# Axial attention on one core: the maximum ahead of the reciprocal, GpSimd copying the turned weights by position, ScalarE scaling three of four strips

## The chip, the core and the metric

The kernel runs on one core of one Trainium2 chip. Its time is the device time of one execution in microseconds (us); of several executions the median is given. The engines are called as in the profile: PE (TensorE), DVE (VectorE), ACT (ScalarE), POOL (GpSimd) and SP (SyncE, which here only issues DMAs). [...]

## The reference

Four layers are computed one after another on an input of 2 x 128 x 128 x 128 (image, channel, row, column) in float32. The change touches the first one alone, an attention along the rows of each column, in eight groups of channels. Cut to what matters:

```python
qkv = _bn(jnp.einsum('bgch,gdc->bgdh', xg, wg), ...)        # per column: q, k (8 each), v (16)
qr = jnp.einsum('bgci,cij->bgij', q, q_emb)                  # q against position embeddings
kr = jnp.einsum('bgci,cij->bgij', k, k_emb).swapaxes(2, 3)
qk = jnp.einsum('bgci,bgcj->bgij', q, k)
sim = _bn(jnp.concatenate([qk, qr, kr], 1), ...).reshape(NW, 3, GROUPS, H, H).sum(1)
sim = jax.nn.softmax(sim, axis=3)
sv = jnp.einsum('bgij,bgcj->bgci', sim, v)                   # weights times values
sve = jnp.einsum('bgij,cij->bgci', sim, v_emb)               # weights times embeddings
so = _bn(jnp.concatenate([sv, sve], -1).reshape(NW, OUT * 2, H), ...)
out = so.reshape(N, W, OUT, 2, H).sum(3)
```

Here `bgij` has one 128 x 128 matrix for each column and group. There are 2 x 128 columns and 8 groups, so 2048 such matrices. A recurrent layer of convolutions, a deformable convolution and a convolution by transforms follow; nothing in them is changed.

## The kernel before, in words

`layer0_prepare` projects q, k and v and stores them in device memory. `layer0_attention` then makes the 2048 matrices. A **unit** is one image, one group and 32 neighbouring columns (64 units). A unit is done in four **pairs** of eight columns each, two rows of `RT` = 4, so there are 256 pairs. One pass of the loop `for m in range(pairs + 14)` handles several pairs at once, each in another phase, and issues the work of all of them in an order written out by hand: the wrapper `InOrder` (line 81 of the kernel, to which the profile books nearly every instruction) keeps each engine's queue in program order. In pass m:

- `logits_pe(u, p)`: PE turns the term `r[0]` into the PSUM tile `lg` (eight transposes) and adds the products of q and k (`lg<-qk`). `add_term`: DVE adds the other term `r[1]` and writes `e` (128 x 1024).
- `maxima`: DVE reduces `e` to the negated maximum `mx` of each row. `exponentials`: ACT applies the exponential in eight pieces, each with its sum into `total`.
- `divide`, one pass later: DVE takes the reciprocal of `total`, POOL multiplies `e` by it.
- `turn`, two passes later: PE transposes the weights `e` in two halves (r = 0, 1) into the PSUM tile `te`, of which there is one buffer. `turned`: ACT copies each half into `u.et`, by position (row, then column). `turned_v`: DVE copies each half into `et`, in the order in which it stands in PSUM.
- `values`, three passes later: PE multiplies `et` by the values `vt` (`po<-et,vt`), and ACT copies the result to `svt`.
- `embedded_pe`, six passes later: PE multiplies `u.et`, by position, by the value embeddings `ve` (`po<-et,ve`, 32 small products a pass), and ACT copies the result to `ste` in `embedded_copy`.
- `terms_pe`: PE makes a quarter of the embedding products of the next unit in the PSUM tile `gen`, which has four strips of 512 elements. `terms_copy` scales them into `r[0]` or `r[1]`: ACT takes strips 2 and 3, DVE then strips 0 and 1.
- `stats`: DVE takes batch statistics (`bn_stats`) of a half of `svt` or `ste`, one each pass. SP loads `zz`, `vt` and `qk` for later units and stores `svt` and `ste`.

The PSUM tiles `gen`, `lg`, `te` and `po` have one buffer each: PE can fill one again only when its readers are done. `po` serves the values and the embeddings in turn. The tile `et` has two buffers and `e` four.

Of the kernel before, what the change touches and what calls it, by code (L numbers as in the profile page):

```python
# [7 lines left out]
F32 = mybir.dt.float32  # L8
# [7 lines left out]
P = 128  # L16
N = 2
S = 128
RT = 4
# [527 lines left out]
def layer0_attention(env, prm, mem, alphas, mv):  # L547
# [12 lines left out]
    pe, dve, act, pool, sync = (  # L560
        InOrder(tc, e) for e in (nc.tensor, nc.vector, nc.scalar, nc.gpsimd, nc.sync)
    )
    ident = env.ident
    HW = WC // 2
    with ExitStack() as ctx:
# [3 lines left out]
        ep = ctx.enter_context(tc.tile_pool(name="at_e", bufs=3))  # L569
# [3 lines left out]
        st_v, st_e = (  # L573
            cp.tile([P, NG, N * NC, 2, 6], F32, name=f"st_so{k}", tag=f"st_so{k}")
            for k in range(2)
        )
# [20 lines left out]
        units = [(n, g, wc) for n in range(N) for g in range(NG) for wc in range(NC)]  # L597
# [28 lines left out]
        def terms_pe(u, t, k):  # L626

            if k == 0:
                u.r[t] = rp.tile([P, WC, S], F32, name=f"r{t}", tag=f"r{t}")
            ps = pp.tile([P, 4, 4, 4, WC], F32, name="gen", tag="gen")  # L630
            for b in range(4):
                for s in range(4):
                    pe.matmul(
                        ps[:, s, b],
                        lhsT=toep[32 * s : 32 * s + 32, t, 4 * k + b, :],
                        rhs=u.z[32 * s : 32 * s + 32, t, :, 4 * k + b, :],
                        start=True,
                        stop=True,
                    )
            return ps  # L640

        def terms_copy(u, t, k, ps, s):

            to = u.r[t].rearrange("p w (s i) -> p s w i", s=4)
            to = to[:, s : s + 2, :, 16 * k : 16 * k + 16]
            here = ps[:, s : s + 2].rearrange("p s b i w -> p s w (b i)")
            scale = alphas[:, u.g, 1 + t : 2 + t]
            if s == 0:
                dve.tensor_scalar(to, here, scale, None, ALU.mult)
            else:  # L650
                act.activation(to, here, AF.Copy, scale=scale)

        def logits_pe(u, p):

            lg = pp.tile([P, 2, RT, S], F32, name="lg", tag="lg")
            for r in range(2):
                for x in range(RT):
                    pe.matmul(
                        lg[:, r, x, :],
                        lhsT=u.r[0][:, (2 * p + r) * RT + x, :],  # L660
                        rhs=ident,
                        is_transpose=True,
                        start=(x == 0),
                        stop=False,
                        skip_group_check=True,
                    )
            for x in range(RT):
                for r in range(2):
                    lo = u.base + 32 * r
                    w = p * RT + x  # L670
                    pe.matmul(
                        lg[:, r, x, :],
                        lhsT=qk[lo : lo + 8, 0, w, :],
                        rhs=qk[lo : lo + 8, 1, w, :],
                        start=False,
                        stop=(x == RT - 1),
                        skip_group_check=True,
                    )
            return lg

        def add_term(u, p, lg):
            e = ep.tile([P, 2 * RT, S], F32, name="e", tag="e", bufs=4)
            dve.tensor_tensor(
                e,
                lg.rearrange("p r x j -> p (r x) j"),
                u.r[1][:, 2 * p * RT : 2 * (p + 1) * RT, :],
                ALU.add,
            )
            return e

        def maxima(e):
            mx = ep.tile([P, 2 * RT], F32, name="mx", tag="mx")
            dve.tensor_reduce(mx, e, AX.X, ALU.max, negate=True)
            return mx
# [13 lines left out]
        def divide(e, total):  # L708
            dve.reciprocal(total, total)
            pool.tensor_tensor(  # L710
                e, e, total.unsqueeze(2).to_broadcast([P, 2 * RT, S]), ALU.mult
            )

        def turn(e, r):

            te = pp.tile([P, RT, S], F32, name="te", tag="te")
            for x in range(RT):
                pe.transpose(te[:, x, :], e[:, r * RT + x, :], ident)
            return te

        def turned(u, p, r, te):
            w0 = (2 * p + r) * RT
            if w0 == 0:
                u.et = rp.tile([P, S, WC], F32, name="et2", tag="et2")
            act.copy(u.et[:, :, w0 : w0 + RT], te.rearrange("p w i -> p i w"))

        def turned_v(et, r, te):
            dve.tensor_copy(et[:, r * RT : (r + 1) * RT, :], te)

        def values(u, p, et):  # L730

# [26 lines left out]
        def embedded_copy(u, k):  # L758
            if k == 0:
                u.sve = sp.tile([P, WC, WC], F32, name="ste", tag="ste")  # L760
            act.copy(u.sve[:, 8 * k : 8 * k + 8, :], po_e)
# [5 lines left out]
        def store_sve(u):  # L767
            for s in range(4):
                sync.dma_start(
                    out=sve[u.g, s, :, u.n, u.wc],  # L770
                    in_=u.sve[32 * s : 32 * s + 16].rearrange("p i w -> p (i w)"),
                )

        def stats(u, st, t, half):
            dve.bn_stats(
                st[:, u.g, u.n * NC + u.wc, half, :],
                t.rearrange("p a b -> p (a b)")[:, 512 * half : 512 * half + 512],
            )
# [4 lines left out]
        pairs = 4 * len(units)  # L783
        us, es, ets, totals = {}, {}, {}, {}
# [3 lines left out]
        for t in range(2):  # L788
            for k in range(2):
                ps = terms_pe(us[0], t, k)  # L790
                for s in (0, 2):
                    terms_copy(us[0], t, k, ps, s)
        for m in range(pairs + 14):
            here = m < pairs
            u, p = us.get(m // 4), m % 4
            nxt = us[m // 4 + 1] if m // 4 + 1 < len(units) else None
            turning = 0 <= m - 2 < pairs
            if here:
                lg = logits_pe(u, p)
                es[m] = add_term(u, p, lg)  # L800
            if m - 1 in totals:
                divide(es[m - 1], totals.pop(m - 1))
            if turning:
                ub, pb = us[(m - 2) // 4], (m - 2) % 4
                e = es.pop(m - 2)
                ets[m - 2] = ep.tile([P, 2 * RT, S], F32, name="et", tag="et", bufs=2)
                te = turn(e, 0)
                turned(ub, pb, 0, te)
                turned_v(ets[m - 2], 0, te)
            if 0 <= m - 3 < pairs:  # L810
                values(us[(m - 3) // 4], (m - 3) % 4, ets.pop(m - 3))
            if here:
                mx = maxima(es[m])
            if nxt and here:
                ps = terms_pe(nxt, p // 2, p % 2)
                for s in (2, 0):
                    terms_copy(nxt, p // 2, p % 2, ps, s)
            piece = m - 6
            if 0 <= piece < pairs:
                embedded_pe(us[piece // 4], piece % 4)  # L820
                embedded_copy(us[piece // 4], piece % 4)
            if turning:
                te = turn(e, 1)
                turned(ub, pb, 1, te)
                turned_v(ets[m - 2], 1, te)
            if here:
                totals[m] = exponentials(es[m], mx)

            for st, k, half in ((st_v, 7, 0), (st_v, 8, 1), (st_e, 10, 0), (st_e, 13, 1)):
                if m >= k and (m - k) % 4 == 0 and (m - k) // 4 < len(units):  # L830
                    done = us[(m - k) // 4]
                    stats(done, st, done.sv if st is st_v else done.sve, half)
            if m % 4 == 3 and m // 4 + 2 < len(units):
                us[m // 4 + 2] = load(m // 4 + 2)
            if m >= 4 and m % 4 == 0 and m // 4 + 1 < len(units):
                load_qk(us[m // 4 + 1])
            if m % 4 == 3 and m >= 7 and (m - 7) // 4 < len(units):
                store_sv(us[(m - 7) // 4])
            if m % 4 == 2 and m >= 10 and (m - 10) // 4 < len(units):
                store_sve(us[(m - 10) // 4])  # L840
            if m % 4 == 1 and m >= 13 and (m - 13) // 4 < len(units):
                us.pop((m - 13) // 4)
        for g in range(NG):
            for k, st in enumerate((st_v, st_e)):
                dve.bn_aggr(mv[:, g, k, :], st[:, g].rearrange("p e f k -> p (e f k)"))
# [1056 lines left out]
```

## Time and profile before

| | us |
|---|---|
| median of 3 executions | 5850.1 |
| lowest and highest | 5849.14, 5858.86 |
| the profiled execution, its time | 5858.64 |
| its span | 5856.4 |
| attention loop, from the first add to the last statistics | about 494 to 2051 |
| one pass of the loop, mean from 700 to 1900 us | 6.01 |

The profile shows one execution. "Busy" is the time in which an engine executes; a line of a timeline gives start, duration, engine, source line, operation, output and inputs, shapes and count, and in brackets the idle time before it with what ended it. A line of the waits gives who waited for whom, the total in us, how often, and the longest. Durations of neighbouring instructions on one engine overlap by about 0.1 us, so the start-to-start time is less than the duration.

### The profile page before, as it was taken

How to read it: one execution, taken by the hardware profiler on the slowest of the kernel's cores; microseconds unless marked ns; L12 is line 12 of the kernel's file. 1: busy time of each engine (PE TensorE's matmuls, PEld its weight loads, DVE VectorE, ACT ScalarE, POOL GpSimd, SP SyncE). 2: the span in 40 equal slices, each digit the busy share in tenths (PEclk: the TensorE clock that was granted, in tenths of full speed). 3: DMA queues.
4: the chain of work that ended last, by engine and by line, in shares of the span. 5: the costliest groups of instructions: out<-in, count | busy, mean ns of one | idle time of the engine just before them, and what ended most of it. 6: DMA issues, size and time to landing. Idle time of an engine off the chain costs nothing. (4 is left out here: it accounts for less than half of the span.)

```text
span 5856.4 us, 162646 instructions
## 1 busy us (share of the span) xinstructions
PE 5399.6 (92%) x67323; PEld 4843.0 (83%) x67323; DVE 3930.1 (67%) x7273; ACT 2784.2 (48%) x8408; POOL 778.5 (13%) x727
## 2 busy tenths in 40 slices
PE   8997999999999804999999999999899999998999
PEld 8866777777777704999999999973799999998888
DVE  3646999999999845555555556653566666666887
ACT  1156999999999845443223330012233333333221
POOL 2112333333333221000000003320000000000000
PEclk9998999999999956999999999999899999999999
DMA  3243222222222284000000001114766777663000
GB/s 143 96 192 98 58 61 58 58 57 57 57 59 59 47 344 155 1 2 1 1 1 1 1 1 44 38 45 124 93 88 88 87 87 89 88 88 55 38 39 40
DMA packets 411365, 401.02 MB, mean 68 GB/s; under 512 B 63232, under 2 KB 368256, under 8 KB 397952
## 3 DMA queue, kind: packets, MB, share of 16 engines
q1 hardware_dynamic: 406160, 380.65, 30.6%
q8 instruction: 541, 8.86, 0.7%
q10 hardware_dynamic: 4464, 9.86, 0.5%
q14 instruction: 200, 1.64, 0.1%
HBM read 251.00 MB, written 139.37 MB: 67 GB/s over the span
## 5 line engine op out<-in xcount | busy, mean ns | idle before, releaser
L81 PE MATMUL pl<-ln,wl 128*128 128x128 f32 (+1 forms) x10160 | 1239.0, 276 | 9.0 <-DVE ln L81 8.2
L81 PEld LDWEIGHTS pl<-ln,wl 128*128 128x128 f32 x10160 | 1175.7, 190 | 20.3 <-issue 7.3
L81 ACT ACTIVATE e<-e,mx 128x128 f32<-128x128 f32 x2048 | 793.6, 395 | 0.4 <-DVE mx L81 0.4
L81 ACT COPY sm<-ps_s 128x432 f32<-128x432 f32 (+1 forms) x768 | 318.4, 487 | 817.3 <-PE ps_s L81 817.3
L81 POOL TENSOR_TENSOR e<-e,total 128x1024 f32<-128x1024 f32 x256 | 485.9, 1898 | 1092.2 <-DVE total L81 1092.2
L81 ACT COPY res<-ln 128x128 f32<-128x128 f32 x762 | 262.7, 345 | 720.1 <-DVE ln L81 720.1
L81 DVE COPY s<-ps_w 100x1152 f32<-100x1152 f32 x256 | 346.5, 1354 | 317.7 <-PE ps_w L81 317.7
L81 PE MATMUL ps_s<-s,xw 100*128 100x144 f32 x4096 | 545.2, 286 | 0.4 <-ACT sm L81 0.3
L81 PE MATMUL po<-sm,wdef 128*128 128x256 f32 x2304 | 539.2, 379 | 0.0
L81 PE MATMUL pl<-ln,ws 128*128 128x128 f32 x4064 | 537.1, 273 | 0.0
L81 PEld LDWEIGHTS ps_s<-s,xw 100*128 100x128 f32 x4096 | 517.2, 190 | 0.9 <-ACT sm L81 0.9
L81 DVE TENSOR_TENSOR v<-pl,c 128x128 f32<-128x128 f32 x508 | 148.2, 292 | 542.7 <-PE pl L81 542.7
L81 PEld LDWEIGHTS pl<-ln,ws 128*128 128x128 f32 x4064 | 494.9, 191 | 0.0
L81 PEld LDWEIGHTS po<-sm,wdef 128*128 128x128 f32 x2304 | 419.8, 190 | 47.6
L81 PE MATMUL m<-x,weff 128*128 128x256 f32 x2048 | 444.2, 380 | 14.8 <-DVE x L81 14.8
L81 PEld LDWEIGHTS m<-x,weff 128*128 128x128 f32 x2048 | 390.4, 191 | 68.3 <-issue 14.8
L81 DVE COPY et<-te 128x512 f32<-128x512 f32 x512 | 351.9, 687 | 85.3 <-ACT et L81 84.7
L81 ACT ACTIVATION_READ_ACCUMULATOR e<-e,mx 128x1 f32 x2048 | 397.7, 194 | 0.0
L81 DVE SCALAR_TENSOR_TENSOR ln<-v,res 128x128 f32<-128x128 f32 x1016 | 343.9, 339 | 49.0 <-DVE v L81 1.3
L81 PE MATMUL te<-cst_main,e 128*128 128x128 f32 x2048 | 334.8, 286 | 41.2 <-DVE et L81 33.8
L81 PE MATMUL gen<-zz,toep 32*128 32x128 f32 x8192 | 333.6, 289 | 19.9 <-DMA zz<-qb_d 12.1
L81 DVE TENSOR_SCALAR r<-gen,alphas 128x1024 f32<-128x1024 f32 x256 | 327.1, 1278 | 28.5 <-DMA qk<-qa_d 14.7
(225 smaller groups left out, 8317.6 us busy)
## 6 DMA issues: line engine op xcount, KB each, us to landing
xw<-px_d SPq DMA_DIRECT2D x1280, 80.0 KB
xa<-in_x SPq DMA_DIRECT2D x16, 1024.0 KB
v_d<-vs SPq DMA_DIRECT2D x16, 1024.0 KB
qb_d<-sb SPq DMA_DIRECT2D x16, 1024.0 KB
qa_d<-sa SPq DMA_DIRECT2D x8, 2048.0 KB
zz<-qb_d SPq DMA_DIRECT2D x1024, 16.0 KB
vt<-v_d SPq DMA_DIRECT2D x64, 256.0 KB
qk<-qa_d SPq DMA_DIRECT2D x256, 64.0 KB
```

Source lines behind the costliest of these rows:

```text
L81: return lambda *a, **k: self.tc.keep_in_program_order(issue(*a, **k))
```

## The change

Three things are changed in the loop, and one follows from them.

- `maxima` stands ahead of `divide`, and both stand after the first `turn` with its copy. Before, the reciprocal came first and the maximum last.
- ACT no longer copies the halves of `te`. DVE's copy of them into `et` is the only reader, and POOL then copies `et` to `u.et`, by position, both halves at once (`by_position`). The embedding products and what comes after them are a pass later, so the loop is one pass longer.
- ACT scales strips 1 to 3 of `gen`, DVE strip 0.
- Of the statistics and stores, those of `ste` move by one pass.

```diff
@@ terms_copy
+            part = slice(0, 1) if s == 0 else slice(1, 4)
             to = u.r[t].rearrange("p w (s i) -> p s w i", s=4)
-            to = to[:, s : s + 2, :, 16 * k : 16 * k + 16]
-            here = ps[:, s : s + 2].rearrange("p s b i w -> p s w (b i)")
+            to = to[:, part, :, 16 * k : 16 * k + 16]
+            here = ps[:, part].rearrange("p s b i w -> p s w (b i)")
@@
-        def turned(u, p, r, te):
-            w0 = (2 * p + r) * RT
-            if w0 == 0:
+        def turned(et, r, te):
+            dve.tensor_copy(et[:, r * RT : (r + 1) * RT, :], te)
+
+        def by_position(u, p, et):
+
+            if p == 0:
                 u.et = rp.tile([P, S, WC], F32, name="et2", tag="et2")
-            act.copy(u.et[:, :, w0 : w0 + RT], te.rearrange("p w i -> p i w"))
-
-        def turned_v(et, r, te):
-            dve.tensor_copy(et[:, r * RT : (r + 1) * RT, :], te)
+            lo = 2 * p * RT
+            pool.tensor_copy(u.et[:, :, lo : lo + 2 * RT], et.rearrange("p w i -> p i w"))
@@ the loop
-        for m in range(pairs + 14):
+        for m in range(pairs + 15):
...
-            if m - 1 in totals:
-                divide(es[m - 1], totals.pop(m - 1))
             if turning:
                 ub, pb = us[(m - 2) // 4], (m - 2) % 4
                 e = es.pop(m - 2)
-                ets[m - 2] = ep.tile([P, 2 * RT, S], F32, name="et", tag="et", bufs=2)
+                et = ep.tile([P, 2 * RT, S], F32, name="et", tag="et", bufs=2)
                 te = turn(e, 0)
-                turned(ub, pb, 0, te)
-                turned_v(ets[m - 2], 0, te)
+                turned(et, 0, te)
+            if here:
+                mx = maxima(es[m])
+            if m - 1 in totals:
+                divide(es[m - 1], totals.pop(m - 1))
             if 0 <= m - 3 < pairs:
                 values(us[(m - 3) // 4], (m - 3) % 4, ets.pop(m - 3))
-            if here:
-                mx = maxima(es[m])
             if nxt and here:
                 ps = terms_pe(nxt, p // 2, p % 2)
-                for s in (2, 0):
+                for s in (1, 0):
                     terms_copy(nxt, p // 2, p % 2, ps, s)
-            piece = m - 6
+            piece = m - 7
...
             if turning:
                 te = turn(e, 1)
-                turned(ub, pb, 1, te)
-                turned_v(ets[m - 2], 1, te)
+                turned(et, 1, te)
+                by_position(ub, pb, et)
+                ets[m - 2] = et
...
-            for st, k, half in ((st_v, 7, 0), (st_v, 8, 1), (st_e, 10, 0), (st_e, 13, 1)):
+            for st, k, half in ((st_v, 7, 0), (st_v, 8, 1), (st_e, 11, 0), (st_e, 14, 1)):
...
-            if m % 4 == 2 and m >= 10 and (m - 10) // 4 < len(units):
-                store_sve(us[(m - 10) // 4])
+            if m % 4 == 3 and m >= 11 and (m - 11) // 4 < len(units):
+                store_sve(us[(m - 11) // 4])
```

More of the change, by code (lines that the diff above doesn't have):

```diff
@@ L790, in layer0_attention @@
                 ps = terms_pe(us[0], t, k)
-                for s in (0, 2):
+                for s in (0, 1):
                     terms_copy(us[0], t, k, ps, s)
-        for m in range(pairs + 14):
+        for m in range(pairs + 15):
             here = m < pairs
@@ L838, in layer0_attention @@
                 store_sv(us[(m - 7) // 4])
-            if m % 4 == 2 and m >= 10 and (m - 10) // 4 < len(units):
-                store_sve(us[(m - 10) // 4])
-            if m % 4 == 1 and m >= 13 and (m - 13) // 4 < len(units):
-                us.pop((m - 13) // 4)
+            if m % 4 == 3 and m >= 11 and (m - 11) // 4 < len(units):
+                store_sve(us[(m - 11) // 4])
+            if m % 4 == 2 and m >= 14 and (m - 14) // 4 < len(units):
+                us.pop((m - 14) // 4)
         for g in range(NG):
```

## The prediction

> **What bounds the kernel now.** First the busy time by stretches. The attention loop runs from about 494 to 2030 us; a stretch inside it reads (stretch, its length, then PE, weight loads, DVE, ACT, POOL busy, granted clock, DMA share, GB/s):
>
> ```profile
> 1000.00:1500.00 500.00, 473.42 (x11982) 394.36 (x11984) 464.23 (x585) 477.10 (x1754) 157.56 (x83) 1.00 0.29 58
> ```
>
> PE, DVE and ACT are each busy 93 to 95%, POOL 32%. No single engine can be read off as the bound, so one pass must be laid out. The timeline of one of the 256 passes (start, duration, engine, operation) shows:
>
> ```profile
> 1205.51 0.63 PE L81 MATMUL po<-et,vt 128*16 128x128 f32 x16
> ...
> 1206.08 1.17 PE L81 MATMUL gen<-zz,toep 32*128 32x128 f32 x32
> ...
> 1206.42 0.58 ACT L81 COPY et<-te 128x512 f32<-128x512 f32 x1
> 1206.56 0.20 DVE L81 RECIPROCAL total<-total 128x8 f32<-128x8 f32 x1
> 1206.88 0.38 ACT L81 COPY svt<-po 128x256 f32<-128x256 f32 x1
> 1206.93 1.90 POOL L81 TENSOR_TENSOR e<-e,total 128x1024 f32<-128x1024 f32 x1 [3.92 <-DVE total L81]
> 1207.03 0.69 DVE L81 COPY et<-te 128x512 f32<-128x512 f32 x1 [0.27 <-ACT et L81]
> ...
> 1207.32 1.12 ACT L81 ACTIVATE r<-gen,alphas 128x1024 f32<-128x1024 f32 x1
> 1207.63 1.21 DVE L81 TENSOR_REDUCE mx<-e 128x8 f32<-128x1024 f32 x1
> ...
> 1208.76 1.28 DVE L81 TENSOR_SCALAR r<-gen,alphas 128x1024 f32<-128x1024 f32 x1
> ```
>
> The reciprocal comes round again at 1212.38, so this pass takes 5.82 us. DVE has no free time in it but two waits: 0.27 us until ACT has read the same `te`, and about 0.1 us for the last exponential. Its own start-to-start steps add to 5.45. ACT is as full: eight exponentials 3.09, two `et` copies 0.47 + 0.48, `svt` 0.26, `r` 1.01, `ste` 0.25 make 5.56. These two hold each other; PE's groups, from start to start without waits, are 0.56 (vt) + 1.23 (gen) + 0.66 (ve) + 0.56 and 0.49 (the two `te`) + 0.97 + 1.09 (`lg`) = 5.56.
>
> The waits between 700 and 1900 us (200 passes) say the same: DVE's copy behind ACT's copy is the largest wait of DVE, and PE in turn waits for both.
>
> ```profile
> POOL e L81 <- DVE total L81: 821.6, 200, 5.8
> DVE et L81 <- ACT et L81: 60.4, 211, 1.2
> ...
> PEld po L81 <- ACT svt L81: 48.5, 146, 0.5
> ...
> PE te L81 <- DVE et L81: 23.5, 126, 0.4
> ```
>
> The 200 passes average 6.01, not 5.82: some PE groups are slower inside than others. `gen` takes 1.17 above but 1.59 at 1217.71; the `ve` group stretches too, up to 1.7 us, in a pattern that repeats every eight passes. Summed over the starts inside the groups, these pauses are 0.25 us per pass. They follow PE's own stream and not the other engines', so they stay. PE alone could therefore do a pass in 5.56 + 0.25 = 5.81.
>
> [...] DVE's copy starts 0.03 us after ACT's ends. In the program as built DVE's `r` also waits for ACT's `r`, before and after. [...] `et` takes 0.69 beside POOL's multiply, 0.68 without; in the merge stage POOL's `res` add takes 2.36 alone and 3.43 beside a DVE add with two SBUF inputs. [...] No row before shows POOL copying.
>
> **The change part by part, per pass.**
>
> *ACT loses the two `et` copies*: −(0.47 + 0.48) = −0.95. DVE's 0.27 wait behind them goes with them, as nobody else reads `te`.
>
> *ACT's `r` grows from 1024 to 1536 elements.* From `svt` (256: 0.37) to `et` (512: 0.58) an element costs 0.8 ns, so +0.43: 1.55 us. If all of it scales, 1.12 × 1.5 = 1.68. I take 1.55. ACT's sum becomes 3.09 + 0.26 + 1.44 + 0.25 = 5.04.
>
> *DVE's `r` falls from 1024 to 512*: the reduce of 1024 against the statistics of 512 (1.21, 0.69) prices 512 elements at 0.52, so 1.28 − 0.52 = 0.76; the copy of that size takes 0.69. I take 0.74. DVE's sum: 0.12 (reciprocal) + 2 × 0.61 + 1.13 + 0.66 + 0.60 + 1.13 = 4.86.
>
> *POOL gains one copy of 1024 elements*, reading with a step of 512 bytes. POOL's rows of 130 and 260 elements (0.465, 0.738) put 0.19 fixed on one. [...] above, the dearest 1024-element row is 3.43. I take 2.7[...]. POOL's pass: 1.90 + 2.7 + two hand-overs of 0.17 (reciprocal end to multiply start, 1206.76 to 1206.93) = 4.9, under PE's 5.81. The `ve` products that need it are moved a pass later, so it has over a pass to end; with `et` in two buffers, the DVE copy two passes on waits for it. It is hidden at any price below about 3.6.
>
> *The maximum goes ahead of the reciprocal*, and the `te` copy ahead of both. The exponentials are fed earlier. What is queued behind: the reciprocal starts about 1.8 us later in DVE's pass, and POOL's multiply with it. That multiply must end before the next pass's first `te`. Counted from the end of `lg`: add 1.13, `et` 0.61, maximum 1.13, reciprocal 0.2, hand-over 0.17, multiply 1.90 = 5.14 against 5.56 to 5.81. It fits, by 0.4 to 0.7.
>
> *A longer wait in the middle of DVE:* `r` now stands behind 1.55 us of ACT. From the start of `gen`: 1.21, ACT `r` 1.59, DVE `r` 0.66, `et` 0.73 to 0.82 (this frees `te`), next `te` 0.56, vt 0.56, next `gen`: 5.31 to 5.40. Also under PE's pass, but by little.
>
> *Statistics:* the embedded half moves by one pass, so of four passes one has two `bn_stats` (0.60 more) and one none. In the double pass DVE's add starts late, and the multiply path becomes 5.14 + 0.6 = 5.7: PE waits then, about 0.2 to 0.6 in one pass of four, partly where PE would have paused anyway. I count 0.04 per pass, 0 to 0.10 as bounds.
>
> *DMA queue (SP):* the four `sve` stores move behind the 16 `zz`, one `vt` and four `sv` issues and ahead of the four `qk`. Their four issues take 2.3 us; `qk` is used three passes later, and `zz` is issued 2.3 earlier. Zero; if that cover were gone, 2.3 per unit of four passes.
>
> *The end:* one more pass of draining, and the last `ve` products wait for POOL's copy: about +2 us once. Prologue copies in the other order: nothing, they wait for PE there.
>
> **Sum.** PE's pass of 5.81 + 0.04 = 5.85 against 6.01: 256 × 0.16 = 41, less 2: 39 us. Against the profiled execution's 5858.6 that is 5820; the median of the runs before stands 8.5 us below it, so I predict **5812**.
>
> **Rivals.**
>
> *PE sets the pass (forecast):* 5.81 to 5.90, −27 to −50 us: 5800 to 5823. For: three sums (ACT 5.04, DVE 4.86, POOL 4.9) fall clear of 5.81. Chance 0.57.
>
> *The pauses shrink too*, because with fewer waits elsewhere they fall under other time: 5.56 to 5.7, −80 to −115 us, 5735 to 5770; halfway, 5785. Against: they lie inside PE's groups. Chance 0.14.
>
> *New waits take it all:* ACT's `r` at 1.68 and hand-overs of 0.17 instead of 0.05 lengthen the `gen`–ACT–DVE–`te` loop to about 5.7, and PE's pauses, which lie in it, add to it: 5.96 to 6.0. About 5840 to 5850. Chance 0.13.
>
> *Slower, POOL becomes the bound:* its queue is in order, so a dear copy delays the next multiply, hence the next `te`. With POOL never idle the hand-overs fall away and the pass is 1.90 + copy. Break-even is a copy of 6.01 − 1.90 = 4.1; at 4.5 the pass is 6.40 and the kernel 256 × 0.39 = +100 us, 5950. For: no row shows this pattern, 128 runs of 8. Against: `res` with runs of 16 took 2.36 alone, 2.1 ns an element, no more than contiguous rows. Chance 0.16, a little of it for DVE being held by POOL after all.
>
> That the change doesn't do what it says is excluded: as built, ACT has 512 copies fewer and POOL 256 more.
>
> **How the numbers follow.** Time 5812, the forecast case. Low 5776 takes in half of the second case; high 5856 takes in the forecast, the lost gain and the mildest of the last. Measurements of this kernel tell about 0.2% (12 us) from no change. Faster by more: 0.57 + 0.14 + 0.02 = 0.73; within: 0.11; slower: 0.16.
>
> **What would show it.** Right: ACT `r` near 1.55 and DVE `r` near 0.74; POOL copies 2 to 3.4 us; no ACT `et`; ACT busy some 87% of the loop and PE 95% or more; passes near 5.85; DVE's largest wait is `r` behind ACT. Wrong: POOL copies over 3.6 with PE's `te` waiting for POOL; or passes of 5.98 with DVE's `r` the wait that ends last; or PE's pauses gone.

## The result, and the profile after

The changed kernel takes 5784.8 us, median of 4 executions (5782.25 to 5788.19), beside 5852.9 of the kernel before: a ratio of 0.9886, 95% interval 0.9871 to 0.9900. It is 68 us faster. The prediction had 38 us and a range that holds 5784.8; the direction and the range were right, the size of the gain was not. The forecast case by itself (5800 to 5823) missed: the range held because its low end took in half of the case of shrinking pauses, which did not come about. That this was enough is luck.

The two profiled executions, 5856.4 and 5783.8 us long, show where the time went. The attention loop, from the first maximum to the last copy of `ste`, falls from 1555.4 to 1488.3 us, by 67.1; what stands between it and the recurrent layer is 234.9 and 235.5, the rest 3570.3 and 3569.7. Another 5.4 us fall before the loop begins (495.7 and 490.3); in the runs below this start lies anywhere from 491 to 497, whatever was changed, so these are not counted as an effect. One pass takes 5.76 us in the mean of 200 passes, where it took 6.01. The stretch inside the loop (columns as before):

```profile
1000.00:1500.00 500.00, 488.41 (x12510) 410.36 (x12504) 428.94 (x608) 448.95 (x1652) 340.08 (x174) 1.00 0.33 61
```

PE is busy 98% now; DVE, ACT and POOL have 14, 10 and 32% to spare. In the kernel before, three engines stood level at 93 to 95%. A pass in the timeline of the changed kernel, one of the short ones (5.47 us to the next `gen`):

```profile
1206.08 1.17 PE L81 MATMUL gen<-zz,toep 32*128 32x128 f32 x32
1206.14 0.68 DVE L81 COPY et<-te 128x512 f32<-128x512 f32 x1
1206.36 0.36 ACT L81 COPY svt<-po 128x256 f32<-128x256 f32 x1
1206.74 1.21 DVE L81 TENSOR_REDUCE mx<-e 128x8 f32<-128x1024 f32 x1
...
1207.18 0.61 PEld L81 LDWEIGHTS po<-et,ve 128*16 128x16 f32 x64
1207.19 0.73 PE L81 MATMUL po<-et,ve 128*16 128x32 f32 x64
1207.33 1.54 ACT L81 ACTIVATE r<-gen,alphas 128x1536 f32<-128x1536 f32 x1 [0.61 <-PE gen L81]
...
1207.87 0.19 DVE L81 RECIPROCAL total<-total 128x8 f32<-128x8 f32 x1
1208.23 1.90 POOL L81 TENSOR_TENSOR e<-e,total 128x1024 f32<-128x1024 f32 x1 [1.38 <-DVE total L81]
...
1208.90 0.75 DVE L81 TENSOR_SCALAR r<-gen,alphas 128x512 f32<-128x512 f32 x1 [0.84 <-ACT r L81]
...
1210.31 2.03 POOL L81 COPY et<-et 128x1024 f32<-128x1024 f32 x1 [0.18 <-DVE et L81]
```

DVE's `et` no longer waits for ACT. ACT's `svt` ends at 1206.72, while `gen` still runs, so the `ve` products follow `gen` at once: 1.11 us after its start. In the pass of the kernel before that the prediction laid out they came 1.23 us after it, and the first of their weight loads says why:

```profile
1207.31 0.61 PEld L81 LDWEIGHTS po<-et,ve 128*16 128x16 f32 x64 [0.26 <-ACT svt L81]
```

The tile `po` is shared: the `ve` products may not overwrite it before ACT has copied the values out of it to `svt`, and ACT copied a half of `te` first. POOL's copy takes 2.03 us. The waits between 700 and 1850 us, again 200 passes:

```profile
DVE r L81 <- ACT r L81: 135.9, 199, 1.1
ACT r L81 <- PE gen L81: 110.9, 200, 1.1
...
PEld te L81 <- POOL e L81: 17.7, 66, 0.5
...
PE te L81 <- POOL e L81: 5.7, 24, 0.3
```

ACT now waits for PE, and DVE for ACT; neither delays PE in most passes. What is left of PE's own waits is the first `te` behind POOL's multiply. The wait of `ve` for `svt`, 48.5 us on the weight loads before, is gone.

**PE's account.** The starts of PE's groups, read from the trace, give one sum for every run below. A group is a run of products into one tile; its step is the time from its first start to that of the next group. Without waits and pauses a pass is 0.56 (vt) + 1.10 (gen) + 0.66 (ve) + 0.56 + 0.49 (`te`) + 0.97 + 1.09 (`lg`) = 5.43 us. To it come the pauses inside groups, the mean delay of `ve` after `gen` beyond its shortest step, and that of the first `te` after `lg`. These two delays are called "late" from here on, and a late pass is one in which the first `te` starts late:

| us a pass | pauses | `ve` late | first `te` late | sum | pass measured |
|---|---|---|---|---|---|
| before | 0.25 | 0.15 | 0.18 | 6.01 | 6.01 |
| changed | 0.27 | 0.00 | 0.06 | 5.76 | 5.76 |

The change took 0.15 us of waiting from `ve` and 0.12 from `te`: less 0.02 of longer pauses, that is 256 × 0.25 = 64 of the 67 us; the rest lies outside these 200 passes.

### The profile page after: what moved, and what is told of

It reads as the page before. It is cut to its first block, busy times and chain, and to the rows that moved or that the text cites. A ratio compares the mean times of both kernels' runs of the same rounds, so it can differ in the third digit from the quotient of the medians.

```text
span 5783.8 us, 162452 instructions
## 1 busy us (share of the span) xinstructions
PE 5374.1 (93%) x67323; PEld 4833.4 (84%) x67323; DVE 3770.7 (65%) x7273; ACT 2638.0 (46%) x7896; POOL 1292.9 (22%) x983
## 5 line engine op out<-in xcount | busy, mean ns | idle before, releaser
L81 POOL COPY et<-et 128x1024 f32<-128x1024 f32 x256 | 518.9, 2027 | 34.9 <-DVE et L81 25.9
L81 ACT ACTIVATE r<-gen,alphas 128x1536 f32<-128x1536 f32 x256 | 395.0, 1543 | 164.7 <-PE gen L81 140.3
L81 POOL TENSOR_TENSOR res<-ln,x1t 128x128 f32<-128x128 f32 x256 | 134.0, 524 | 1484.4 <-DVE ln L81 1484.4
L1653 POOL MEMSET col<- 128x10 f32 x32 | 3.7, 116 | 1867.5 <-ACT weff L1633 1488.3
```

The costliest lines, as they stand in the source:

```text
L81: return lambda *a, **k: self.tc.keep_in_program_order(issue(*a, **k))
L1653: nc.gpsimd.memset(cols[0][:, :, 0:1], 0.0)
```

## The experiments

All edits are to the changed kernel unless the text says otherwise. Medians of 4 or 5 executions stand beside the kernel before on the same chip (5849.0 to 5853.4), with the ratio to it. The 95% interval of a ratio is about ±0.0016, or 9 us, so times alone hardly tell two kernels apart that differ by less than some 13 us and were timed on different chips. Where the differences are that small, the waits in the traces have to agree.

**The copy alone.** The other two edits undone.

```diff
-            part = slice(0, 1) if s == 0 else slice(1, 4)
+            part = slice(0, 2) if s == 0 else slice(2, 4)
...
                 es[m] = add_term(u, p, lg)
+            if m - 1 in totals:
+                divide(es[m - 1], totals.pop(m - 1))
...
-            if here:
-                mx = maxima(es[m])
-            if m - 1 in totals:
-                divide(es[m - 1], totals.pop(m - 1))
...
+            if here:
+                mx = maxima(es[m])
             if nxt and here:
```

> The change with the reciprocal first and the strips two and two again, so that only the copy to POOL (and the pass that the embedding products moved) is left. Theory A, the copy's move freed PE and the other two edits add little or nothing: the pass is 5.70 to 5.78 us, the kernel within 8 us of the changed one (5777 to 5793 us). Theory B, the three edits add up, each taking off part of the 68 us: ACT keeps 5.1 us and DVE 5.5 us of work a pass and the pass is 5.85 to 5.92, so 5810 to 5830 us.

Measured 5790.6 us, 0.9895 (0.9879 to 0.9912); pass 5.78; `ve` late 0.00, first `te` late 0.10. Moving the copy brings 62 us, nearly all of the gain. The wait for `svt` goes with it alone. The kernel still has the embedding products and their statistics a pass later; no run delays only these. In the kernel before, `po` waits for no engine's data but `svt`, so the delay by itself would not have removed that wait (argued, not run), and `copy_spread` below shows that undoing the shift of the statistics changes nothing here (5789.5).

**The reciprocal first.** As above, but with the strips left at one and three.

> The change with the reciprocal ahead of the maximum again; copy on POOL, strips one and three. Theory A: the reorder of the maximum puts the reciprocal and with it POOL's multiply 1.7 us later in DVE's pass and makes PE's te wait for POOL in the pass with two statistics; undone, that wait goes: pass 5.66 to 5.70, kernel 5760 to 5775 us, faster than the changed one. Theory B: the exponentials are fed later, ACT waits for the maximum, pass 5.80 to 5.85, 5795 to 5810 us.

Measured 5770.8 us, 0.9861 (0.9844 to 0.9877): 14 us below the changed kernel, in theory A's range, though the pass of 5.73 is above its 5.66 to 5.70. The two ratios' intervals overlap a little (the changed kernel has 0.9871 to 0.9900), but the traces agree: the first `te` is late by 0.02 instead of 0.06. In the changed kernel the last thing to end before a late `te` is POOL's multiply, in 68 of 73 late passes; here it is DVE's second `et` copy in all of 39. The reorder of the maximum costs time here.

**Strips two and two.** Only the first hunk of the first experiment.

> The change with the strips two and two again. Theory A: DVE gains 0.52 us of work but waits 0.45 us less for ACT, so nothing or a little: pass 5.76 to 5.80, kernel 5785 to 5798 us. Theory B: the shift of a strip was worth a third of the gain, 20 us or more: 5805 us and over.

Measured 5797.3 us, 0.9905 (0.9888 to 0.9921); pass 5.81, first `te` late 0.12. That is 12.5 us above the changed kernel, at the upper end of what theory A gave. With the reciprocal first the same shift is worth more: `copy_alone` and `recip_first`, timed on one chip, differ in the strips alone, and by 19.8 us. So the shift of a strip is worth 12 to 20 us, and theory A ("nothing or a little") is too low. The order of the maximum costs 7 us with two and two strips (this run beside `copy_alone`, passes of 5.81 and 5.78). In 122 of the 157 late passes the last thing to end before `te` is DVE's second `et` copy, in the other 35 POOL's multiply; the waits of this run show the latter:

```profile
PEld te L81 <- POOL e L81: 27.9, 94, 0.5
```

**One statistics instruction a pass.**

```diff
-            for st, k, half in ((st_v, 7, 0), (st_v, 8, 1), (st_e, 11, 0), (st_e, 14, 1)):
+            for st, k, half in ((st_v, 7, 0), (st_v, 8, 1), (st_e, 10, 0), (st_e, 13, 1)):
```

> The change with the statistics of the embedded half in the passes in which they stood before, so one statistics instruction in each pass and never two. Theory A: the pass of 6.13 us, in which te waits for POOL's multiply, falls to 5.6 to 5.7, the pass of 5.14 rises to 5.5; mean 5.66 to 5.70, kernel 5760 to 5775 us. Theory B: the 6.13 comes from PE's own pauses, which stay: within 5 us of the changed kernel.

Measured 5777.2 us, 0.9875 (0.9858 to 0.9891); pass 5.72, first `te` late 0.03. The passes of a unit, by their medians, go from 5.30, 5.51, 5.69, 6.13 to 5.82, 5.50, 5.50, 5.61: the long pass of 6.13 is from the statistics, not from PE's pauses. The mean fell less than forecast, since the short pass gave most of it back, and the 7.6 us by which the kernel is below the changed one are not told from noise by the times alone.

**The maximum first, in the kernel before,** and nothing else:

```diff
-            if m - 1 in totals:
-                divide(es[m - 1], totals.pop(m - 1))
...
                 turned_v(ets[m - 2], 0, te)
+            if here:
+                mx = maxima(es[m])
+            if m - 1 in totals:
+                divide(es[m - 1], totals.pop(m - 1))
...
-            if here:
-                mx = maxima(es[m])
             if nxt and here:
```

> The kernel before with the maximum and the first te copy ahead of the reciprocal, nothing else. Theory A: ACT still copies te, so DVE still waits for it, and the later multiply delays te: pass 6.05 to 6.10, slower than before by 12 to 25 us (5862 to 5878 us). Theory B: the exponentials start earlier and ACT's pass shortens: 5.85 to 5.95, faster than before by 15 to 40 us.

Measured 5876.3 us, 1.0042 (1.0028 to 1.0056): slower by 23. DVE waits longer behind ACT, and `te` behind the later multiply:

```profile
DVE et L81 <- ACT et L81: 114.0, 192, 0.9
PEld te L81 <- POOL e L81: 88.2, 166, 0.8
```

What holds PE is the second: the first `te` is late by 0.36 us a pass instead of 0.18, and POOL's multiply ends last before it in 165 of 167 late passes.

**Strips one and three, in the kernel before,** and nothing else (the lines of `terms_copy` as in the change).

> The kernel before with ACT taking three strips and DVE one, nothing else. Theory A: ACT with its two te copies has 5.98 us of work in a pass and becomes the bound: pass 6.08 to 6.15, slower than before by 20 to 35 us (5870 to 5890 us). Theory B: DVE set the pass and is relieved of 0.52 us: 5.7 to 5.9, faster by 25 us or more.

Measured 5874.4 us, 1.0036 (1.0022 to 1.0050): slower by 21. While ACT copies `te`, the third strip brings it to 5.98 us of work a pass by the estimate above; `svt` comes late, and `ve` is late by 0.44 us a pass.

```profile
PEld po L81 <- ACT svt L81: 105.8, 183, 0.9
PE po L81 <- ACT svt L81: 67.0, 139, 0.7
```

So two of the three edits lose 21 to 23 us each by themselves. In the changed kernel the strip gains, and the maximum still costs.

**POOL's copy twice.**

```diff
-            pool.tensor_copy(u.et[:, :, lo : lo + 2 * RT], et.rearrange("p w i -> p i w"))
+            for _ in range(2):
+                pool.tensor_copy(u.et[:, :, lo : lo + 2 * RT], et.rearrange("p w i -> p i w"))
```

> The changed kernel with POOL's copy by position issued twice (4.06 us instead of 2.03), the same result. The rival of the prediction in which POOL becomes the bound: 1.90 + 4.06 = 5.96 a pass and hand-overs, 5.97 to 6.10, so 5845 to 5880 us. If POOL is as free as its 1.7 us of idle time suggests and only its sum counts: 5.96 or less. If the second copy is hidden altogether: 5785 us.

Measured 5833.8 us, 0.9970 (0.9957 to 0.9984); pass 5.93, so 5845 to 5880 was missed and "only its sum counts" came true. POOL is hardly ever idle (15 of 1150 us), and `te` waits for it: 0.30 us a pass.

```profile
L81 POOL COPY et<-et 128x1024 f32<-128x1024 f32 x389 | 788.3, 2027 | 14.5 <-DVE et L81 2.6
L81 POOL TENSOR_TENSOR e<-e,total 128x1024 f32<-128x1024 f32 x194 | 369.3, 1904 | 0.2
```

The rival of a POOL bound is real, and its break-even lies about where the prediction had it: with 4.05 us of copying, the sum of 1.90 + 4.05 = 5.95 comes to the measured pass, still just under the 6.01 of before. The hand-overs that I added in the expectation do not count once POOL has work waiting.

**Half of the embedding products.**

```diff
-                for s in range(4):
+                for s in range(0, 4, 2):
```

> The changed kernel without half of the embedding products (two of four row strips of ve, 16 instead of 32 small products a pass): 0.33 us of PE work and an eighth of its instructions less. That part of the output is left out. If PE sets the pass: 5.40 to 5.55, 256 x 0.2 to 0.33 = 50 to 85 us less, 5700 to 5735 us. If the wait for POOL's multiply and the chain of ACT's and DVE's r behind gen set most of it: 5.62 to 5.68, 20 to 35 us less, 5750 to 5765 us.

Measured 5752.0 us, 0.9827 (0.9812 to 0.9843): 33 us less than the changed kernel, not the 50 to 85 expected of a kernel that PE alone sets. The 0.33 us of the expectation was wrong, though, and so was its eighth of PE's instructions (64 of 288 in a pass go). The step of `ve` falls from 0.66 to 0.58 only, since the products overlap: a set of four instructions, each about 0.20 us long, starts every 29 to 33 ns in the changed kernel, and a set of two every 29 ns here. What falls more are the pauses, from 0.27 to 0.11. PE's account is 5.43 − 0.08 + 0.11 = 5.46, which is 0.24 less than in the changed kernel, or 62 us. But the pass is 5.63, as the first `te` is now late by 0.17: it is late in all 204 passes, behind POOL's multiply in 104 and behind DVE's second `et` copy in 100. So the next bound, the chain through ACT, DVE and POOL, lies at about 5.6, close under PE's 5.7.

**Combinations.** `rf_spread` joins the edits of the experiments on the reciprocal and on the statistics. `copy_spread` is the same with the strips two and two. `after_again` is the changed kernel once more. Their expectations, in this order:

> Both undone that helped alone: reciprocal first, and one statistics instruction in each pass; copy on POOL, strips one and three. Theory A, PE's own pass (groups 5.43 us and pauses 0.28) is the floor, and each of the two already reached it (5.73, 5.71): they do not add up, pass 5.69 to 5.72, kernel 5763 to 5772 us. Theory B, two separate waits, which add up: 5.65 to 5.68, 5750 to 5760 us.

> The copy's move alone, with the statistics in the passes of before: reciprocal first, strips two and two. Theory A, the strips' share is worth nothing once PE is the floor: pass 5.69 to 5.73, kernel 5763 to 5776 us, and the 17 us more of copy_alone were the double statistics. Theory B, DVE with 0.52 us more work is a bound of its own: as copy_alone, 5785 to 5792 us.

> The changed kernel once more beside the two others of this call: 5785 us, within 5 us.

The three ran on one chip. `rf_spread` took 5770.7 us, 0.9860 (0.9844 to 0.9877), pass 5.71; `copy_spread` 5789.5, 0.9893 (0.9877 to 0.9910), pass 5.78; the changed kernel 5780.4, 0.9879 (0.9862 to 0.9895), pass 5.75. Theory A holds for `rf_spread`: the gains do not add, since PE's 5.43 and 0.27 of pauses leave next to nothing more to take. It fails for `copy_spread`. With two strips on DVE the passes even out but their mean stays, and the first `te` is late by 0.09. In that kernel DVE's second `et` copy ends within 0.15 us before `te` in 155 of the 156 late passes; in `rf_spread` only 38 passes are late at all. The two differ by 18.9 us, and in the strips alone. The chain from `gen` over ACT's `r`, DVE's `r` and the `et` copy to the next `te` is what these point to: its two `r` steps, with a hand-over of 0.03, are 1.15 + 1.20 = 2.35 us with two and two strips and 1.58 + 0.67 = 2.25 with one and three. Of the 0.10 between them 0.07 appears in the first `te` (0.09 and 0.02) and in the pass (5.78 and 5.71).

The reciprocal first with strips one and three is the best version that was run: 5770.7 to 5770.8 us, with or without the spread statistics, some 10 to 14 us below the changed kernel.

## Why the prediction was right, and where its size was off

- **What bounds it before: right in kind.** ACT, DVE and PE hold each other, and ACT's two copies are what binds them; `copy_alone`, 62 us faster, shows it.
- **PE's own pass: this term was mis-sized.** I read 1.23 us for `gen` as a step without waits, from the quickest passes. Nearly all of those held a wait of `ve` for ACT's `svt`; the line of `PEld po` waiting for `svt`, which I showed, named it. Of 200 passes before, `gen` paused inside in 50, and in none of these did `ve` wait; in 146 of the other 150 it did. Free of both the step is 1.10 (median in every run that has the copy on POOL). So PE's floor was 5.43 + 0.25 = 5.68 and not 5.81: 0.13 × 256 = 33 us that were counted as PE's own work and were a wait that the change removes. Pauses and `te` each came out 0.02 longer than predicted, which takes 10 back; the 5 us left of the gap between the 39 predicted and the 67 of the loop lie outside the 200 passes.
- **The pauses stay: right.** They went from 0.25 to 0.27 us. The half of `ve` products showed that they belong to PE's stream: those inside `ve` vanish with half the products, and all of them together fall from 0.27 to 0.11 us a pass. In the changed kernel 30 pauses between 700 and 1850 us are longer than 0.4 us, and they make up about half of the whole. Each ends 1.2 to 1.9 us after a transfer of 16 KB on the queue of instructions has ended, most of them 1.3 to 1.6 us after, where random instants would be spread over the 5.2 us between two such transfers. The kernel before has 22 such pauses and the same distance. What PE waits for there no trace shows, and no run tests it. The page of the changed kernel lists this queue for the whole execution (packets, MB, share of the DMA engines):

```profile
q8 instruction: 541, 8.86, 0.7%
```

- **ACT −0.95, ACT's `r` 1.55, DVE's `r` 0.74: right,** measured 1.54 and 0.75.
- **POOL's copy at 2.7: too dear,** it took 2.03. The 2.7 was my own estimate, and nothing in the kernel before showed it. With the 0.19 fixed, itself an estimate from the rows of 130 and 260 elements, 2.03 us make an estimated 1.8 ns an element, beside 1.7 for the multiply's 1.90. As the copy is hidden at either price, no time hung on it.
- **The maximum, costed at nothing but a fit of 0.4 to 0.7 us: too kind.** In the double pass the multiply is late, as foreseen, and the first `te` waits 0.06 us a pass where I had 0.04. Undoing the reorder gives 7 to 14 us. Taken by itself in the kernel before, it cost 23.
- **The rivals.** The second rival's halfway figure, 5785, is what was measured, but not for its reason: the pauses did not shrink, and what shrank was the step that I had counted as wait-free. The POOL bound was named with a break-even of 4.1 us, and doubling the copy came within 20 us of it. The third rival, the new chain through `r`, exists, but lies under PE's pass: with two strips on DVE it seems to be what costs the 12 to 20 us.
- **A small reading.** The loop ends at 2052 us and not at 2030; no term of the sum rests on it.

## What to carry to other kernels

When several engines are level, take the wait-free step of each group from a pass in which nothing it depends on was late; the quickest passes of a coupled loop can nearly all hold the same wait, as 146 of 150 did here. Relieve the engine that couples the others first: of the two edits that lost 21 and 23 us alone, the strip gained 12 to 20 us once ACT was free, and the maximum lost only 7 to 14. And a copy on an engine that idles two thirds of the time was free here at 2.03 us, and cost time once the engine's sum came up to the pass.

## What the runs showed of the hardware

POOL copies 1024 float32 elements, reading with a step of 512 bytes and writing runs of 8, in 2.03 us (changed), and its multiply of the same size takes 1.90 before and after. DVE's operations in this loop keep their durations beside POOL's work: `et` takes 0.68 us with and without it in the changed kernel (0.69 and 0.68 before), the add 1.22 beside it (changed) and 1.21 alone (before), the maximum 1.21 beside the multiply (before) and alone (changed). With half of the embedding products PE starts two instructions every 29 ns, where it starts four every 29 to 33 ns with all of them, and leaving out half of the strips took only 0.08 of 0.66 us.
